# A transformer block on one core: fewer warming products, other ranks for an order written by hand, a table loaded first, and a last group in two banks

## The chip, the cores and the metric

The kernel runs on one core of one Trainium2 chip. The time is device microseconds (us) of one execution. Before the change the median of three runs is 572.95 us (572.05 to 573.83). A core has five engines with queues of their own: TensorE (PE), VectorE (DVE), ScalarE (ACT), GpSimd (POOL) and SyncE (SP), which here issues nearly all DMA transfers.

## The reference

The input `x` is 4 x 2048 x 256, float32. The block adds an attention-like part and then a feed-forward part (FFN), each on a normalized x:

```python
x = x + attn(layernorm(x))
x = x + ffn(layernorm(x))

# attn: u, v of 256 channels each
u, v = split(silu(xn @ uv_w))
a    = Toeplitz coefficients, 4096 lags x 256 channels, from a small network
y    = irfft(rfft(a) * rfft(v), n=4096)[:2048]
attn = (u * y) @ o_w

# the network: position -> 32 features
h = pos @ rpe_pos_w
for i in range(3):
    h = silu(ln(h)) @ rpe_fc_w[i]
a = silu(ln(h)) @ rpe_out_w          # times 0.99 ** |lag|

# ffn: 8 groups of 1024 tokens, each with its own weights, no function in between
h1 = x_g @ W1[g].T + b1[g]           # 256 -> 1024
h2 = h1 @ W2[g].T + b2[g]            # 1024 -> 256
```

As nothing stands between the two products of the FFN, the kernel multiplies W1 and W2 with each other first (`pw`, a 256 x 256 result per group, kept in `wt`) and then applies `wt` to the tokens (`pff`).

## The kernel before, in words

**An order written out by the kernel itself.** The stages don't call the engines. They call a `Recorder`, which notes every instruction as an `Operation` with a *rank*. `at(key, b)` sets the rank: `place(key, b)` looks the key up in the table `PLACE` (L156), which gives 20 x b plus the entry. For the first batch the key with " first" behind it goes ahead, for the last batch the key with " last". A key that is not there falls back to its parent: "w.3.l.1" to "w.3.l", that to "w.3", that to "w". When all is recorded, `issue_order` (L289) writes the order: it keeps a simple model of the time of each operation (`Operation.cost`), of the buffers of each pool, and again and again takes the operation that can start first by that model, of several the one of lowest rank. The result goes to the engines in that order, under `tc.manual_schedule()`. Each engine's queue then runs in order, and waits on semaphores where data or a buffer is missing. So a rank only moves instructions past each other within what the data and the buffers allow; and all recorded instructions have one line in the profile, L1166, and are told apart by their tiles.

**The stages**, for a batch b of 4, a quarter q of 4 (512 tokens each) and a half h of 2 (128 channels each):

- *Warming products*, keys "warm.i" (L1123): `zeros` (128 x 256) times itself, into the bank of `ps_w`; nothing reads the result. There are `WARM_UP` = 20 of them, and each has a rank of its own. A 128x256 float32 product is two instructions in the profile.
- `rpe_network` (keys "rpe...", L628): SP loads parameters, lags and the first two quarters of x that are used (q = 0 and 2); the two halves of quarter 0 go by ACT's queue. Then four layers, each in two halves k: the product `ph`, its square `sq` and copy `d` on ACT, the variances `pvar` (16 small products), three Newton steps for the inverse root on DVE (`nt`, `ny`), its spread `ne`, four transposes `pr`, a product with `d` on DVE, and Silu on ACT (`z`). Each step needs the one before it. Then `pz`, the last transposes.
- `stage_a` (keys "a.q..."): x is normalized (`xn_a`), transposed (`pt_a`, copied to `xnt` by ACT), multiplied (`pv`), Silu on ACT gives `v`, and POOL makes the sums and differences `c` of the convolution. For the first batch these fill PE while the network's steps wait on each other.
- `stage_w` (keys "w.g...", L854), for each of the 8 FFN groups: four pairs of loads `w1`, `w2` of 256 KB each ("w.g.l.i"), each in a ring of `WB` = 3 buffers; ACT adds a bias in place; then 8 instructions of `pw` for the pair ("w.g.m.i"). All 32 gather in one bank, as `ps_w` has a single one, and DVE takes it out to `wt` ("w.g.s"). A buffer comes free when `pw` has used it, and the next load then takes its place; the next group can start only when the bank is out.
- `rpe_transform` (keys "rpet..."): the network's result is transformed to the coefficients `am` that the convolution multiplies with: `hp`, then `pa`, row-tiled (products with 64 rows, at two `tile_position`s), 8 of them under each of the four keys "rpet.1.a" to "rpet.7.a".
- `prepare` ("p.h.n"): the butterflies of the convolution on DVE, ahead of `stage_b` ("f.h.r..." forward product `pf` and multiplication `y` with `am`; "b.h.r..." backward product `acc`; "e.h.n" the butterflies behind it, then the product with the gate on POOL). Its tables `mats` are loaded anew for each r, in rings of 3 buffers.
- `gate` ("g.h.q"): the product `pu` and its Silu.
- `stage_d` ("d.q...", L1068): `po` (the output projection), added to x, normalized, transposed (`pt_d`, copied to `xn` by ACT), the FFN's product `pff` in two groups j of 256 tokens, added to x by DVE, and stored. For the last batch the `pff` groups are in the two banks of `ps_i` (tag "acc"), and each group has a store of 256 KB of its own. Quarter 1 is the last to be done.

The eight PSUM banks are: `ps_f` 2, `ps_i` 2, `ps_w` 1, `ps_mm` 3. Silu and the simple functions of ACT (copy, square, identity) need a table, which the profile shows as ACT_TABLE_LOAD.

Of the kernel before, what the change touches and what calls it, by code (L numbers as in the profile page):

```python
# [31 lines left out]
F32 = mybir.dt.float32  # L32
I32 = mybir.dt.int32
AF = mybir.ActivationFunctionType
ALU = mybir.AluOpType
# [106 lines left out]
class Pool:  # L142
# [14 lines left out]
    "a.0": 1.74, "a.0.t": 0.0,  # L157
    "a.1": -2.67, "a.1.c": 26.0, "a.1.t": -5.0, "a.1.v": -1.3,
    "a.2": 2.51, "a.2.c": 101.0, "a.2.n": 6.0, "a.2.v": 3.0,
    "a.3": 5.3, "a.3.c": 31.0, "a.3.t": 4.46, "a.3.x": 1.0,  # L160
    "a.0.c first": -99.0, "a.0.n first": -160.0, "a.0.t first": -150.0, "a.0.v first": -122.0, "a.0.x first": -190.0, "a.0.w first": -142.0,
    "a.1 first": -98.0, "a.1.c first": -98.0, "a.1.t first": -112.0, "a.1.v first": -111.0,
    "a.2.c first": -124.0, "a.2.n first": -152.0, "a.2.t first": -120.0, "a.2.v first": -119.0,
    "a.2.x first": -140.0,
    "a.3 first": -96.0, "a.3.c first": -96.0, "a.3.t first": -104.0, "a.3.x first": -96.0,
    "b.0": 13.79, "b.0.0": 6.26, "b.0.0.p": 5.0, "b.0.1.m": 12.16, "b.0.1.p": 12.0, "b.0.1.y": 8.0, "b.0.2": 4.1,
    "b.0.2.y": 18.0, "b.0.3.m": 8.11, "b.0.3.p": 6.0, "b.0.3.y": 6.6, "b.0.4.m": 8.37, "b.0.4.p": 11.0,
    "b.0.4.y": 7.0, "b.0.6": 12.58, "b.0.6.p": 12.0, "b.0.7": 14.11, "b.0.7.y": 13.0,
    "b.1": 10.46, "b.1.0.p": 8.0, "b.1.1": 20.27, "b.1.1.y": 32.0, "b.1.2.m": 87.0, "b.1.2.p": 17.0,
    "b.1.2.y": 15.97, "b.1.3": 19.01, "b.1.3.p": 16.0, "b.1.4.m": 18.94, "b.1.4.p": 18.0, "b.1.4.y": 143.0,  # L170
    "b.1.5": 18.98, "b.1.5.y": 19.0, "b.1.6": 20.74, "b.1.6.p": 21.3, "b.1.7": 20.97, "b.1.7.p": 21.4,
    "b.0 last": 4.1, "b.0.0.p last": 2.0, "b.0.0.y last": 15.0, "b.0.1 last": 12.16, "b.0.1.p last": 7.3,
    "b.0.1.y last": 12.16, "b.0.2.y last": 4.1, "b.0.3.p last": 7.0, "b.0.3.y last": 6.0, "b.0.4.p last": 2.3,
    "b.0.4.y last": 2.0, "b.0.5.m last": 13.79, "b.0.5.p last": 7.1, "b.0.5.y last": 9.0, "b.0.6.p last": 12.58,
    "b.0.6.y last": 220.0, "b.0.7.y last": 20.0,
    "b.1 last": 27.0, "b.1.0.m last": 10.46, "b.1.0.p last": 7.0, "b.1.0.y last": 18.0, "b.1.1.m last": 77.0,
    "b.1.1.p last": 27.0, "b.1.1.y last": 120.0, "b.1.2 last": 15.97, "b.1.2.m last": 15.97, "b.1.2.p last": 15.97,
    "b.1.2.y last": 20.0, "b.1.3.p last": 20.7, "b.1.3.y last": 21.0, "b.1.4.p last": 20.0, "b.1.4.y last": 53.0,
    "b.1.5.y last": 27.0, "b.1.6.m last": 92.0, "b.1.6.p last": 32.7, "b.1.6.y last": 57.0, "b.1.7.p last": 47.0,
    "b.1.7.y last": 64.0,  # L180
    "d.w": -60.0,
    "d.0": 27.7, "d.0.n": 27.0, "d.0.o": 25.35, "d.0.x": 25.35,
    "d.1": 28.74, "d.1.n": 27.0, "d.1.o": 26.25, "d.1.x": 26.25,
    "d.2": 30.44, "d.2.f": 36.0, "d.2.s": 33.54, "d.2.t": 33.54,
    "d.3": 31.46, "d.3.n": 29.38, "d.3.o": 29.15, "d.3.x": 29.38,
    "d.0 last": 42.27, "d.0.f last": 111.0, "d.0.n last": 42.27, "d.0.o last": 97.0, "d.0.t last": 63.0,
    "d.0.x last": 42.27,
    "d.1 last": 140.66, "d.1.n last": 184.0, "d.1.o last": 145.0, "d.1.x last": 65.21,
    "d.2.f last": 59.0, "d.2.n last": 154.0, "d.2.o last": 100.0, "d.2.t last": 79.0, "d.2.x last": 46.22,
    "d.3.f last": 85.0, "d.3.n last": 178.0, "d.3.o last": 104.0, "d.3.t last": 100.0, "d.3.x last": 61.26,  # L190
    "e.0": 14.0, "e.0.0": 14.31, "e.0.1": 26.0, "e.0.3": 15.0, "e.0.4": 63.85, "e.0.5": 71.2, "e.0.6": 77.59,
    "e.0.7": 13.0, "e.0.10": 22.0,
    "e.1.0": 21.0, "e.1.1": 20.5, "e.1.2": 41.0, "e.1.3": 39.0, "e.1.4": 21.4, "e.1.5": 39.89, "e.1.6": 22.0,
    "e.1.7": 25.0, "e.1.8": 22.6, "e.1.9": 27.0, "e.1.10": 28.0,
    "e.0 last": 22.0, "e.0.1 last": 18.21, "e.0.2 last": 18.05, "e.0.3 last": 16.77, "e.0.7 last": 22.0,
    "e.0.9 last": 21.84, "e.0.10 last": 21.0,
    "e.1.0 last": 85.0, "e.1.1 last": 100.83, "e.1.2 last": 37.0, "e.1.3 last": 79.0, "e.1.4 last": 154.0,
    "e.1.5 last": 229.0, "e.1.6 last": 100.0, "e.1.7 last": 60.0, "e.1.8 last": 74.0, "e.1.9 last": 104.0,
    "e.1.10 last": 122.0,
    "f.0": 2.91, "f.0.0": 2.08, "f.0.0.p": 3.0, "f.0.2.m": 1.13, "f.0.2.p": -1.7, "f.0.2.y": 0.0, "f.0.3.m": 2.05,  # L200
    "f.0.3.p": -1.0, "f.0.3.y": 4.0, "f.0.4": 4.0, "f.0.4.p": 7.0, "f.0.5.m": 3.57, "f.0.5.p": 6.0, "f.0.5.y": 9.0,
    "f.0.6.m": 101.0, "f.0.6.p": 11.7, "f.0.6.y": 5.0, "f.0.7.m": 7.2, "f.0.7.p": 10.0, "f.0.7.y": 7.0,
    "f.1": 18.04, "f.1.0.m": 81.0, "f.1.0.p": 7.0, "f.1.0.y": 4.04, "f.1.1.m": 18.16, "f.1.1.p": 13.4,
    "f.1.1.y": 16.0, "f.1.2.m": 13.91, "f.1.2.p": 12.3, "f.1.2.y": 10.0, "f.1.3.m": 14.02, "f.1.3.p": 12.0,
    "f.1.3.y": 10.0, "f.1.4.m": 14.8, "f.1.4.p": 14.0, "f.1.4.y": 11.0, "f.1.5": 14.19, "f.1.5.y": 13.0,
    "f.1.6.m": 17.79, "f.1.6.p": 17.7, "f.1.6.y": 13.43,
    "f.0 last": 0.0, "f.0.0 last": 0.0, "f.0.0.m last": 2.08, "f.0.0.p last": 0.0, "f.0.1.m last": 2.91,
    "f.0.2 last": 1.13, "f.0.2.p last": 1.13, "f.0.2.y last": 4.0, "f.0.3 last": 2.05, "f.0.3.p last": 2.05,
    "f.0.3.y last": 2.05, "f.0.4.p last": 4.0, "f.0.4.y last": 3.0, "f.0.5.m last": 33.0, "f.0.5.p last": 7.0,
    "f.0.5.y last": 6.0, "f.0.6 last": 6.5, "f.0.6.m last": 6.5, "f.0.6.p last": 10.0, "f.0.6.y last": 6.5,  # L210
    "f.0.7.m last": 45.0, "f.0.7.p last": 9.4, "f.0.7.y last": 6.26,
    "f.1 last": 14.02, "f.1.0 last": 4.04, "f.1.0.m last": 4.04, "f.1.0.p last": 9.0, "f.1.1 last": 18.16,
    "f.1.1.p last": 20.3, "f.1.1.y last": 18.16, "f.1.2 last": 13.91, "f.1.2.p last": 12.0, "f.1.2.y last": 13.91,
    "f.1.3.p last": 14.02, "f.1.3.y last": 14.02, "f.1.4 last": 14.8, "f.1.4.p last": 14.8, "f.1.4.y last": 14.8,
    "f.1.5.y last": 16.0, "f.1.6.p last": 32.0, "f.1.6.y last": 24.0, "f.1.7.m last": 18.04, "f.1.7.p last": 52.0,
    "f.1.7.y last": 55.0,
    "g.0.0": 7.0, "g.0.1": 6.5, "g.0.2": 15.0, "g.0.3": 5.68,
    "g.1.0": 24.0, "g.1.1": 9.2, "g.1.2": 20.0, "g.1.3": 21.0,
    "g.0.0 first": -95.0, "g.0.1 first": 1.77, "g.0.2 first": -51.0, "g.0.3 first": -40.12,
    "g.1.0 first": -72.0, "g.1.1 first": -63.0, "g.1.2 first": -20.0, "g.1.3 first": -56.0,  # L220
    "p.0": 5.0, "p.0.0": 112.0, "p.0.1": 1.74, "p.0.2": 22.08, "p.0.3": 23.91, "p.0.4": 1.63, "p.0.5": 110.0,
    "p.0.6": 38.78, "p.0.8": 4.06, "p.0.9": 16.19, "p.0.11": 33.43, "p.0.12": 39.59, "p.0.13": 95.0, "p.0.14": 8.0,
    "p.0.15": 33.61,
    "p.1.0": 14.03, "p.1.1": 11.0, "p.1.2": 11.32, "p.1.3": 67.54, "p.1.4": 106.0, "p.1.5": 15.0, "p.1.6": 14.31,
    "p.1.7": 12.0, "p.1.8": 15.07, "p.1.9": 18.9, "p.1.10": 70.61, "p.1.11": 20.64, "p.1.12": 55.0, "p.1.13": 20.4,
    "p.1.14": 45.22, "p.1.15": 23.0,
    "p.0.0 first": 21.76, "p.0.1 first": -58.0, "p.0.2 first": -38.0, "p.0.3 first": -3.8, "p.0.4 first": -3.5,
    "p.0.5 first": -23.28, "p.0.6 first": -84.19, "p.0.7 first": -2.6, "p.0.8 first": -26.0, "p.0.9 first": -2.0,
    "p.0.10 first": -21.0, "p.0.11 first": -9.0, "p.0.12 first": -1.1, "p.0.13 first": -0.8, "p.0.14 first": -0.5,
    "p.0.15 first": -8.0,  # L230
    "p.1.1 first": 5.6, "p.1.4 first": 11.67, "p.1.5 first": 16.0, "p.1.7 first": 16.92, "p.1.8 first": 31.0,
    "p.1.10 first": 73.0, "p.1.12 first": 26.0, "p.1.15 first": 86.73,
    "rpe": -145.0,
    "rpe.0": -180.0,
    "rpe.1": -150.0,
    "rpe.2": -135.0,
    "rpe.3": -132.0,
    "rpe.d": -174.0,
    "rpe.s": -179.0,
    "rpe.v": -170.0,  # L240
    "rpe.z": -100.0,
    "rpet": -82.0,
    "rpet.0": -33.0, "rpet.0.m": -10.0,
    "rpet.1": -26.0, "rpet.1.a": -50.0, "rpet.1.m": -10.0,
    "rpet.2": -23.0, "rpet.2.m": -10.0,
    "rpet.3": -77.0, "rpet.3.a": -9.6, "rpet.3.m": -10.0,
    "rpet.4": -65.0, "rpet.4.m": -10.0,
# [1023 lines left out]
```

## Time and profile before

| | |
|---|---|
| median of 3 runs | 572.95 us (572.05, 572.95, 573.83) |
| the profiled execution | 572.52 us |
| its span, from the first instruction to the last | 570.6 us |
| granted TensorE clock over the span | 1.000 |
| first matmul starts | 1.19 us |
| last add on DVE starts | 567.02 us |
| DMA | 81.37 MB, mean 143 GB/s |
| `w` loads: 64 of 256 KB, median from issue to landing | 4.4 us |
| `mats` loads: 128 of 256 KB | 2.7 us |
| stores of 512 KB, 256 KB | 2.9 us, 2.0 us |

The busy time of the engines by stretches of the span, in us:

| stretch | what is in it | PE | DVE | ACT | POOL |
|---|---|---|---|---|---|
| 0 to 50 | the network, first stage a, groups 0 and 1 of w | 47.1 | 30.0 | 37.3 | 16.1 |
| 50 to 160 | the transform, gate, first convolution | 110.0 | 103.2 | 52.0 | 25.1 |
| 160 to 520 | the batches | 358.3 | 337.0 | 204.8 | 98.9 |
| 520 to 570.6 | last weights, last stage d | 45.1 | 35.1 | 17.7 | 9.8 |

How to read it: busy time of PE contains overlap of pipelined instructions, so a stretch with 110.0 of 110 us may still hold waits below a microsecond. A line of the timeline has the start, the duration from the first start to the last end of a row of like instructions, the engine, the line, the operation with its output and input tiles, how many, and in brackets the idle time ahead of it with what ended it.

### The profile page before, as it was taken

What the parts mean: (1) busy time and instruction counts of PE and PEld (TensorE: products, weight loads), DVE (VectorE), ACT (ScalarE), POOL (GpSimd) and SP (SyncE); (2) the same over time, 40 slices, a digit from 0 to 9 for tenths busy, and PEclk for the clock granted to TensorE, in tenths of its full rate; (3) what the DMA queues carried; (4) which work ended last, traced back from release to release, by engine and by line L of the source; (5) the groups of instructions that cost most, each with busy time, mean ns of one, the idle gap of its engine ahead of it and who ended that gap; (6) DMA issues with size and microseconds to landing.
All of it is one profiled execution on the core that took longest, in us unless ns stands there. A gap on an engine that the chain in (4) does not pass through costs nothing.

```text
span 570.6 us, 8345 instructions
## 1 busy us (share of the span) xinstructions
PE 560.5 (98%) x2676; PEld 459.8 (81%) x2676; DVE 505.3 (89%) x1122; ACT 311.7 (55%) x820; POOL 149.8 (26%) x184
## 2 busy tenths in 40 slices
PE   9999999999999999999999999999999999999997
PEld 6778667988887788888788788887887888878785
DVE  7646998999997999999968999999959999989963
ACT  3987772533333824868756618868568237112162
POOL 1245120020534320204473010316462021020410
PEclk9999999999999999999999999999999999999999
DMA  8832673544574326365251454545332553434212
GB/s 292 273 89 57 189 225 119 185 130 139 175 176 148 86 109 204 118 215 202 76 147 51 138 184 129 187 160 162 111 74 93 158 193 109 140 130 118 67 38 111
DMA packets 40483, 81.37 MB, mean 143 GB/s; under 512 B 5876, under 2 KB 7412, under 8 KB 40440
## 3 DMA queue, kind: packets, MB, share of 16 engines
q1 hardware_dynamic: 39960, 80.19, 45.4%
q10 hardware_dynamic: 480, 0.66, 0.3%
q8 instruction: 21, 0.34, 0.2%
q14 instruction: 22, 0.18, 0.1%
HBM read 72.44 MB, written 8.39 MB: 142 GB/s over the span
## 4 chain that ended last, share of the span: by engine, by line
PE 95%; DVE 2%; DMA 1%; ACT 1%; issue 0%; SPq 0%; ACTq 0%; DVEq 0%
PE acc L1166 18%; PE pf L1166 18%; PE pff L1166 10%; PE pu L1166 10%; PE po L1166 9%; PE pv L1166 9%; PE pw L1166 8%; PE pt_a L1166 2%; PE pt_d L1166 2%; PE warm L1166 2%; PE pa L1166 1%; DMA w<-in_L_ffn_W_dram 1%; PE hp L1166 1%; PE ph L1166 1%; PE pvar L1166 1%; PE pr L1166 1%
## 5 line engine op out<-in xcount | busy, mean ns | idle before, releaser
L1166 PE MATMUL acc<-mats,y 128*128 128x256 f32 (+1 forms) x512 | 114.5, 367 | 0.0
L1166 PEld LDWEIGHTS acc<-mats,y 128*128 128x128 f32 x512 | 91.8, 190 | 15.7 <-issue 3.9
L1166 POOL TENSOR_TENSOR gt<-gt,tk 128x512 f32<-128x512 f32 x32 | 44.9, 1416 | 114.9 <-DVE tk L1166 114.8
L1166 PE MATMUL pw<-w,w 128*128 128x256 f32 x256 | 62.5, 381 | 2.5 <-ACT w L1166 1.3
L1166 POOL TENSOR_TENSOR c<-v 128x256 f32<-128x256 f32 x64 | 51.3, 827 | 50.4 <-ACT v L1166 36.3
L1166 PE MATMUL pu<-xnt,uvw 128*128 128x512 f32 x128 | 61.0, 594 | 0.0
L1166 PE MATMUL pv<-uvw,xnt 128*128 128x256 f32 x256 | 61.0, 380 | 0.0
L1166 PE MATMUL po<-ow,gt 128*128 128x256 f32 x256 | 60.6, 380 | 0.3 <-DVE xd L1166 0.3
L1166 PE MATMUL pff<-wt,xn 128*128 128x256 f32 x256 | 59.5, 382 | 0.7 <-ACT xn L1166 0.7
L1166 PE MATMUL pf<-ra,mats 128*128 128x256 f32 x256 | 59.5, 379 | 0.0
L1166 PEld LDWEIGHTS pw<-w,w 128*128 128x128 f32 x256 | 46.7, 190 | 12.0 <-ACT w L1166 3.6
L1166 PEld LDWEIGHTS pff<-wt,xn 128*128 128x128 f32 x256 | 48.0, 190 | 8.4 <-ACT xn L1166 2.1
L1166 ACT ACTIVATE w<-w,dw 128x256 f32<-128x256 f32 x64 | 29.4, 501 | 46.1 <-DMA w<-in_L_ffn_W_dram 46.0
L1166 PEld LDWEIGHTS pv<-uvw,xnt 128*128 128x128 f32 x256 | 48.1, 190 | 7.8 <-issue 1.2
L1166 PEld LDWEIGHTS pf<-ra,mats 128*128 128x128 f32 x256 | 48.4, 190 | 7.1 <-PE po L1166 0.2
L1166 PEld LDWEIGHTS po<-ow,gt 128*128 128x128 f32 x256 | 47.5, 190 | 8.1 <-DVE xd L1166 1.2
L1166 DVE TENSOR_TENSOR y<-y,far 128x256 f32<-128x256 f32 x128 | 53.1, 453 | 0.1
L1166 POOL TENSOR_TENSOR rs_d<-ve_d,mhalf 128x4 f32<-128x4 f32 x16 | 19.0, 1188 | 113.0 <-ACT ve_d L1166 95.9
L1166 POOL TENSOR_TENSOR rs_a<-ve_a,mhalf 128x4 f32<-128x4 f32 x16 | 20.2, 1262 | 106.0 <-ACT ve_a L1166 92.2
L1166 ACT COPY e<-acc 128x512 f32<-128x512 f32 x24 | 14.0, 582 | 53.1 <-PE acc L1166 52.2
L1166 ACT ACTIVATE gt<-pu 128x512 f32<-128x512 f32 x32 | 19.0, 593 | 40.8 <-PE pu L1166 38.4
L1166 DVE TENSOR_TENSOR y<-pf,am 128x512 f32<-128x512 f32 x56 | 38.2, 682 | 3.5 <-PE pf L1166 3.4
(159 smaller groups left out, 1042.4 us busy)
## 6 DMA issues: line engine op xcount, KB each, us to landing
mats<-in_mats_dram SPq DMA_DIRECT2D x128, 256.0 KB, 2.7
w<-in_L_ffn_W_dram SPq DMA_DIRECT2D x64, 256.0 KB, 4.4
xa<-in_x_dram SPq DMA_DIRECT2D x16, 512.0 KB, 4.6
xd<-in_x_dram SPq DMA_DIRECT2D x14, 512.0 KB, 3.6
out_dram<-xd SPq DMA_DIRECT2D x12, 512.0 KB, 2.9
mats_rpe<-in_mats_dram SPq DMA_DIRECT2D x8, 256.0 KB, 4.5
row<-in_L_ffn_b_dram SPq DMA_DIRECT2D x8, 128.0 KB, 4.8
ph<-in_phases_dram SPq DMA_DIRECT2D x8, 128.0 KB, 5.1
```

Of the source, the lines that this page charges most:

```text
L1166: ops[k].call(*ops[k].args, **ops[k].kw)
```

## The change

There are four edits.

1. `WARM_UP` is 11 instead of 20: nine warming products fewer.
2. One ACTIVATE more, Silu of `eps` (128 x 1) into a tile that nothing reads. It has the rank of the first warming product, so it stands near the head of ACT's queue.
3. In `stage_d`, for the last batch, quarter 1, group j = 1: instead of one `pff` tile of two 256-column halves, one add and one store of 256 KB, there are two tiles (both of tag "acc"), each with its two products, its own add of 256 columns and its own store of 128 KB.
4. `PLACE` has 473 keys instead of 445: 177 keys have another value, 225 the same, 43 are gone and 71 are new.

```diff
-    "a.0.c first": -99.0, "a.0.n first": -160.0, "a.0.t first": -150.0, "a.0.v first": -122.0, "a.0.x first": -190.0, "a.0.w first": -142.0,
...
+    "a.0.c first": -99.0, "a.0.n first": -214.0, "a.0.t first": -158.0, "a.0.v first": -156.0, "a.0.w first": -142.0,
+    "a.0.x first": -190.0,
...
-    "rpe": -145.0,
+    "rpe": -152.0,
     "rpe.0": -180.0,
-    "rpe.1": -150.0,
-    "rpe.2": -135.0,
-    "rpe.3": -132.0,
+    "rpe.1": -175.0,
+    "rpe.2": -159.0,
+    "rpe.3": -150.0,
     "rpe.d": -174.0,
     "rpe.s": -179.0,
-    "rpe.v": -170.0,
+    "rpe.v": -240.0,
...
-    "rpet.1": -26.0, "rpet.1.a": -50.0, "rpet.1.m": -10.0,
...
-    "rpet.3": -77.0, "rpet.3.a": -9.6, "rpet.3.m": -10.0,
+    "rpet.1": -65.0, "rpet.1.a": -23.4, "rpet.1.m": -10.0,
...
+    "rpet.3": -59.0, "rpet.3.a": -22.0, "rpet.3.m": -10.0,
...
-    "w.3": 32.0, "w.3.l.0": -27.0, "w.3.l.1": 2.0, "w.3.l.2": 34.0, "w.3.l.3": 14.0, "w.3.m.1": 25.0, "w.3.m.2": 3.0,
-    "w.3.m.3": 21.0, "w.3.s": 36.0,
...
+    "w.3": 32.0, "w.3.l.0": 1.0, "w.3.l.1": 2.0, "w.3.l.2": 34.0, "w.3.l.3": 14.0, "w.3.m.1": -8.0, "w.3.m.2": 17.0,
+    "w.3.m.3": 21.0, "w.3.s": 3.0,
...
-COLD, IDLE, WARM_UP = 3500, 1800, 20
+COLD, IDLE, WARM_UP = 3500, 1800, 11
...
         for j in range(2):
+            if last and q == 1 and j == 1:
+
+                for i in range(2):
+                    t = 2 * j + i
+                    pf = ps_i.tile([P, D], F32, tag="acc", name=f"pff_{b}_{q}_{t}")
+                    for dt in range(2):
+                        T.matmul(pf, xn2[:, dt, t * P : (t + 1) * P], wt[:, dt, :], start=(dt == 0), stop=(dt == 1))
+                    V.tensor_tensor(xt[:, t, :], xt[:, t, :], pf, ALU.add)
+                    S.dma_start(out[b, q][:, t, :], xt[:, t, :])
+                continue
...
     V.memset(zeros, 0.0)
+
+    A.activation(const.tile([P, 1], F32, name="silu0"), eps, AF.Silu)
     warm = ps_w.tile([P, 2, D], F32, tag="w", name="warm")
```

The other ranks of `PLACE` that change belong to the same stages (a, b, d, e, f, g, p, rpe, rpet, w) and are not printed here. Since `issue_order` works on all operations at once, they move instructions throughout the program; the prediction names the places that matter to it, by the position of an instruction in its engine's order.

## The prediction

> **What bounds the kernel now.** I read the page first, then the chain of waits, then the timeline of each place where the chain leaves TensorE (PE), and last the order in which the changed program's instructions stand on each engine.
>
> ```profile
> span 570.6 us, 8345 instructions
> ...
> PE 560.5 (98%) x2676; PEld 459.8 (81%) x2676; DVE 505.3 (89%) x1122; ACT 311.7 (55%) x820; POOL 149.8 (26%) x184
> ...
> PE 95%; DVE 2%; DMA 1%; ACT 1%; issue 0%; SPq 0%; ACTq 0%; DVEq 0%
> ```
>
> The set-up is simple: 95% of the chain that ends last is PE. Time can only go away in two ways: fewer products, or fewer waits of PE. Busy PE is pipelined, so I count starts: in a stream, one 128x256 instruction starts every 0.216 us (16 of `pv` take 3.45 us in the chain of waits), a 128x512 one every 0.429, a 128x128 one every 0.109. By these prices all PE instructions of the old program make 549.6 us. From the first start (1.19) to the slot after the last (566.75) 565.6 us pass, so PE loses about 16 us; then 3.8 us of tail. Where the 16 are:
>
> ```profile
> 1.19 6.63 PE L1166 MATMUL warm<-zeros 128*128 128x256 f32 x20 [1.19 <-DVE zeros L1166]
> ...
> 14.48 1.28 ACT L1166 ACT_TABLE_LOAD   x1
> 15.77 1.52 ACT L1166 ACTIVATE z<-d,par 128x512 f32<-128x512 f32 x2
> ...
> 16.64 1.98 PE L1166 MATMUL ph<-z,bd 128*128 128x512 f32 x4 [1.07 <-ACT z L1166]
> ```
>
> The first 20 instructions of `warm` take 6.6 us instead of 4.3: the first ten run at half speed, the other ten at full speed. Then the network of four layers is a latency chain, and its second layer (`ph<-z,bd`) waits for Silu's table. The wait printed is 1.07; counted by starts it is 1.24, since the pipeline's end covers a part. At the third layer's `pr`, 0.29 and 0.65 us go the same way (starts at 38.3 and 39.5, behind DVE's `ne`).
>
> ```profile
> 173.52 7.56 SPq L1166 DMA_DIRECT2D w<-in_L_ffn_W_dram  x8
> ...
> 177.31 0.91 ACT L1166 ACTIVATE w<-w,dw 128x256 f32<-128x256 f32 x2 [7.62 <-DMA w<-in_L_ffn_W_dram]
> ...
> 178.25 1.97 PE L1166 MATMUL pw<-w,w 128*128 128x256 f32 x8 [1.34 <-ACT w L1166]
> ...
> 199.65 0.70 PE L1166 MATMUL pff<-wt,xn 128*128 128x256 f32 x2 [0.40 <-ACT xn L1166]
> ```
>
> A weight buffer's turn: PE lets it go at 173.3, SP issues the loads at 173.5, ACT adds the bias at 177.3, PE uses it at 178.25: 4.95 us. The order had put only 3.45 us of products in between (8 products, two instructions each), so PE waited 1.50. The `pff` at 199.65 had 0.44 us of products between its transposes and itself, and waited another 0.57.
>
> ```profile
> 526.43 5.95 PE L1166 MATMUL pw<-w,w 128*128 128x256 f32 x24 [0.43 <-issue]
> ...
> 533.10 1.97 PE L1166 MATMUL pw<-w,w 128*128 128x256 f32 x8 [0.71 <-DMA w<-in_L_ffn_W_dram]
> ```
>
> The last group of weights: 0.59 us until the single bank of `pw` is evacuated (two `po` products, 0.86 us, stood there as cover: the evacuation takes 1.45), then 0.19, 0.20 and 0.88 us for three buffers with 4.31, 4.31 and 3.45 us of products as cover. With the waits that fall into them, these turns took 4.7 to 5.3 us.
>
> **The change part by part.**
>
> *Nine products of zeros fewer.* 18 instructions at 0.216 = 3.88 us of PE work. In the new order ten products still stand ahead of `ph0` (so the warming up is as before) and one behind it; the nine that go stood between 9 and 27 us, where the chain of the network was waited for. They are worth 3.88 only if that chain gets shorter too.
>
> *The table, and the start's new order.* One load instead of two: 1.28 us less in ACT's queue right ahead of `z`. I followed the new order with the old rows' durations. Newton's steps for layer 0 are no longer mixed with three BN_STATS (0.42 each), so `ne` starts at 10.4 instead of 10.9; `pr` stands right behind the transposes, 11.3 instead of 12.6; two products with `d` (0.69) and `z` (0.81) follow, `z` at 12.8 instead of 15.8, `ph1` at 13.8, `pvar1` ends at 17.8 instead of 22.8. Layers 2 and 3 by the same rows (Newton 2.5, `ne` 0.68, `z` 0.81, two ACT copies and squares 0.5 each) bring `pz`, the network's end, to 48.5; it was at 54.7. Products ahead of `pz`: 42.5 us in the new order, 48.5 in the old. So PE loses 6.0 us up to there, before 6.2: the 1.24 of the table and that 0.94 at `pr` go, and new ones come where zeros had filled in: 0.5 ahead of the first transposes, 0.8 at `pv` of quarter 2 (0.44 of products as cover for a copy of 0.59 and two hops), 0.5 at `ph3`, and crumbs. One cost is new: Silu on `eps` and its table load now stand between the two loads of the first x on ACT's queue. Before, the second was issued at 1.19; now between 1.2 (if the queue runs past a table load) and 2.5. It landed 3.8 us after its issue, and DVE wants it at 5.66: 0 to 0.85 us late, and w0, `ph0` and the chain behind it with it. No row shows a DMA issue behind a table load; I take 0.4. Start: -0.2 + 0.4 = +0.2 (bounds -1.5 and +2).
>
> *Row-tiled products in fewer groups.*
>
> ```profile
> 74.56 0.59 PE L1166 MATMUL pw<-w,w 128*128 128x256 f32 x2
> 75.09 1.13 PE L1166 MATMUL pa<-wz,tr 64*128 64x256 f32 x8
> ```
>
> Going into `pa` and out again costs 0.39 us by starts (0.10 in, 0.20 inside, 0.10 behind). The old order does it five times, the new one three: -0.78.
>
> *Weight loads.* In the new order groups 3 and 2 are laid out otherwise: the covers in products are 5.60, 4.74, 9.48 and 4.74 us, and 1.29 for the evacuation. Against 4.95 and 1.45 these wait 0.2 three times: 0.6 instead of 1.50, -0.9. In the first 50 us one buffer has 5.16, enough if its turn is no longer than the 4.7 to 5.3 seen. At the end the evacuation has one product as cover, 0.43: it waits 1.02 instead of 0.59, and the buffers behind keep their waits, as their covers (3.88, 3.88, 3.45) and that wait together are the old ones: +0.43. The `pff` at 199.65 gets 1.30 us of cover: -0.57. The `mats` loads are covered by 3.9 us or more in both, but for one with 3.45 at 366; at 3.9 none waited: nothing taken.
>
> *The FFN's last group.*
>
> ```profile
> 565.30 0.69 DVE L1166 TENSOR_TENSOR xd<-xd,pff 128x512 f32<-128x512 f32 x1 [2.59 <-PE pff L1166]
> 567.02 0.69 DVE L1166 TENSOR_TENSOR xd<-xd,pff 128x512 f32<-128x512 f32 x1 [1.04 <-PE pff L1166]
> ```
>
> The last add works on 256 columns (0.41 for such an add out of PSUM at 200.46) instead of 512 (0.69): -0.28. The last store is 128 KB, issued as before from SP; 512 KB take 2.9 us, 256 KB 2.0, so 128 KB between 1.55 and 2.0, I take 1.85: -0.15. One more DMA (0.33 of SP) lies under the products. Against it: the third half-tile needs the bank that the add of 565.30 to 565.98 frees, and its slot was 565.89: +0.2. Sum -0.2 (bounds -0.6 and +0.1).
>
> *All other ranks* move equal work about. DVE is 95% busy from 60 to 160 us, so a stage there could turn DVE-bound; but its work begins with `pz`, 6 us earlier, and PE comes only 4 us earlier. A new wait can cost 0 to 3 us in all; taken 0.5.
>
> Sum: -3.88 + 0.2 - 0.78 - 0.9 - 0.57 + 0.43 - 0.2 + 0.5 = -5.2. The profiled execution took 572.52 (its span and 1.9 around it) and becomes 567.3; the median of the runs is 572.95, 0.43 more: 567.7.
>
> **The Trainium skill.** "ScalarE: Activation LUTs", section "What ACT_TABLE_LOAD costs", gives about 1283 ns for the load and some 1380 ns of drain, an estimate of 2.66 us per switch; here the load is 1.283, but `z` starts 0.01 us behind it, so by the page the sum would be 1.4 us lower, and the trace speaks against it. "TensorE: Matmul & The Clock Gate", section "Why this matters for your kernels", warns of gaps over about 3 us, which bring the half clock back; that speaks against taking zeros out, though no gap in this trace is longer than 1.5 us.
>
> **The rivals.**
> 1. *The zeros only filled waits.* If the network's chain holds `pz` at 52.4 or later, the 3.88 is not gained: 567.7 + 3.9 = 571.6. For it: the zeros stood just where PE had nothing. Against: the chain loses the table, three BN_STATS and the zeros themselves from ahead of `pr` and `pvar`.
> 2. *Slower: weight buffers come late.* The new order uses four buffers with covers of 4.7 to 5.6 us where the old had 11 or more, and PE and ACT stand behind each in order. While the load queue is deep, the first weights took 6.6 to 7.5 us to land (issued 5.42, landed 12.78). With a turn of 7 us instead of 4.95 the four wait 1.8 + 1.4 + 2.3 + 2.3 = 7.8 instead of 0.6: 567.7 + 7.2 = 574.9. It decides from a turn of 6.3 on. Against: by 50 us the old queue had run empty, and turns at 173 and 520 took 4.7 to 5.3.
> 3. *Half clock again at the start.* With gaps between 9.6 and 13 us the clock might fall; instructions then start every 0.427 instead of 0.216 as at 1.19 to 5.3, where it cost 2.1 us: 569.8. Against: the gaps are 0.5 us each.
> 4. *Better:* the new waits of the start and of the rest do not come (-0.2 - 0.4 - 0.5 - 0.6 more): about 565.5.
>
> **How the numbers follow.** Forecast (566 to 569.5) 0.55; better 0.17; half clock, or the late second half of x in full (569.5 to 571.2) 0.11; zeros gain nothing 0.09; slower 0.08. A measurement of this kernel tells about 0.3% (1.7 us) from no change: faster 0.83, same 0.10, slower 0.07. The range reaches from the better case, with the start's lower bound, 564.3, to rival 1, 571.6; it leaves out the slower case.
>
> **What would show it.** `pz` near 48.5 and one table load; `ph1` waiting for z by less than 0.3; three groups of `pa`; waits under 0.5 at the `pw` of groups 2 and 3 near 165; 1.0 us ahead of `pw` near 520; the last store near 1.85 us. `pz` after 52, or a wait over 1.5 at a `pw`, would show it wrong.

## The result, and the profile after

| | before | after |
|---|---|---|
| median | 573.0 us (572.05 to 573.83, 6 runs) | 569.6 us (568.75 to 570.41, 6 runs) |
| ratio of the medians, 95% interval | | 0.9932 [0.9919, 0.9945] |
| the profiled execution, its span | 572.52, 570.6 us | 568.75, 567.0 us |

The change makes the kernel 3.4 us faster. I had predicted 567.7, that is 5.2 less than before.

First the page of the changed kernel: the span, the busy time of the engines and the chain that ended last.

```profile
span 567.0 us, 8316 instructions
...
PE 557.0 (98%) x2658; PEld 455.7 (80%) x2658; DVE 504.5 (89%) x1123; ACT 309.5 (55%) x820; POOL 153.5 (27%) x184
...
PE 77%; DVE 11%; DMA 6%; ACT 3%; issue 1%; SPq 1%; ACTq 0%; DVEq 0%
```

PE has 18 instructions fewer, but the chain that ends last is only 77% PE now, where it was 95%. The chain follows a wait back through the load or the DVE work that ended it, so this share says where the chain passes and not how long PE waited: PE is busy for 98% of the span in both. How long PE waited is counted by starts below.

The timeline of ACT and of PE at the start, in the changed kernel:

```profile
1.19 1.28 ACT L1183 ACT_TABLE_LOAD   x1 [1.19 <-PEq L1272]
1.26 0.38 ACTq L1183 DMA_DIRECT2D xa<-in_x_dram  x1
2.48 0.20 ACT L1183 ACTIVATE silu<-eps 128x1 f32<-128x1 f32 x1
```

```profile
13.60 1.88 PE L1183 MATMUL ph<-z,bd 128*128 128x512 f32 x4
...
48.24 1.04 PE L1183 MATMUL pz<-ident,z 128*128 128x128 f32 x8
```

The last two lines are of PE. The row of `pz` in the kernel before:

```profile
54.70 1.04 PE L1166 MATMUL pz<-ident,z 128*128 128x128 f32 x8
```

There is one table load, and `ph` of the second layer has no wait in brackets any more. `pz`, the end of the network, starts at 48.24 (predicted 48.5, before 54.70). The second load of x stands behind the Silu in ACT's order, but it is issued at 1.26, while the table is still loading (1.19 to 2.47).

To see where the rest went I count what PE has lost at a place: the start of an instruction, less the work that stands ahead of it in PE's order at the prices of the prediction. The column "difference" is what the stretch adds to the loss after, less what it adds before. A place is good to about 0.1 us, since it depends on the prices.

| stretch | loss before, at its ends | loss after, at its ends | difference | predicted |
|---|---|---|---|---|
| products of zeros (work, not loss) | | | -3.88 | -3.88 |
| start to `pz` | 0 to 6.19 | 0 to 5.75 | -0.44 | +0.2 |
| to behind the last group of `pa` | 6.19 to 8.62 | 5.75 to 8.00 | -0.18 | -0.78 |
| to the end of the first batch's `acc` | 8.62 to 9.12 | 8.00 to 9.32 | +0.82 | rest, +0.5 |
| to the first `acc` of batch 1, h = 1 (groups 2 and 3, the `pff` at 199) | 9.12 to 11.63 | 9.32 to 10.51 | -1.32 | -1.47 |
| to `acc` r = 5 of the last convolution | 11.63 to 13.32 | 10.51 to 12.28 | +0.08 | rest |
| to behind the start of the last `acc` | 13.32 to 13.37 | 12.28 to 13.48 | +1.15 | rest |
| `pw` of group 7 | 13.37 to 15.45 | 13.48 to 16.03 | +0.47 | +0.43 |
| to the last quarter's `pff` | 15.45 to 17.06 | 16.03 to 17.38 | -0.26 | rest |
| from there to the end of the span | 7.38 us | 7.33 us | -0.05 | -0.2 |
| around the span | 1.95 us | 1.79 us | -0.16 | 0 |
| sum | | | -3.77 | -5.2 |

Of the -0.44 at the start, 0.27 is the start of `ph` of layer 0 alone (7.48 for 7.75), which depends on when the half rate at the start ends; from there to `pz` the loss fell by 0.17. The wait for a weight buffer near 166 and the wait for the evacuated bank near 523 stand in PE's timeline after:

```profile
166.07 1.97 PE L1183 MATMUL pw<-w,w 128*128 128x256 f32 x8 [0.68 <-DMA w<-in_L_ffn_W_dram]
...
523.12 3.77 PE L1183 MATMUL pw<-w,w 128*128 128x256 f32 x16 [0.88 <-issue]
```

The largest line that I had not foreseen is the last `acc`. The timeline of ACT and of PE there, after:

```profile
515.80 0.91 ACT L1183 ACTIVATE w<-w,dw 128x256 f32<-128x256 f32 x2 [14.78 <-DMA w<-in_L_ffn_W_dram]
516.62 0.56 ACT L1183 COPY e<-acc 128x512 f32<-128x512 f32 x1
```

```profile
515.29 1.03 PE L1183 MATMUL pw<-w,w 128*128 128x256 f32 x4
517.23 1.99 PE L1183 MATMUL acc<-mats,y 128*128 128x256 f32 x8 [0.92 <-ACT e L1183]
```

and the timeline of ACT in the kernel before:

```profile
518.32 0.58 ACT L1166 COPY e<-acc 128x512 f32<-128x512 f32 x1 [8.08 <-PE acc L1166]
520.25 0.91 ACT L1166 ACTIVATE w<-w,dw 128x256 f32<-128x256 f32 x2 [1.35 <-DMA w<-in_L_ffn_W_dram]
```

ACT took these instructions in the order in which they stand. Before, the copy `e` out of the bank of `acc` stood ahead of the bias addition; in the new order it stands behind it. The bias waits for its load until 515.8, while the `acc` that `e` copies had its last product started at 515.1. The next `acc` waits for `e`. By starts this costs 1.08 and another 0.11 for the pipeline to fill.

### The profile page after: what moved, and what is told of

It is laid out like the page before. It is cut to its first block, busy times and chain, and to the rows that moved or that the text cites. A ratio compares the mean times of both kernels' runs of the same rounds, so it can differ in the third digit from the quotient of the medians.

```text
span 567.0 us, 8316 instructions
## 1 busy us (share of the span) xinstructions
PE 557.0 (98%) x2658; PEld 455.7 (80%) x2658; DVE 504.5 (89%) x1123; ACT 309.5 (55%) x820; POOL 153.5 (27%) x184
## 4 chain that ended last, share of the span: by engine, by line
PE 77%; DVE 11%; DMA 6%; ACT 3%; issue 1%; SPq 1%; ACTq 0%; DVEq 0%
PE acc L1183 15%; PE pf L1183 15%; PE pff L1183 10%; PE po L1183 10%; PE pu L1183 7%; PE pv L1183 7%; PE pw L1183 6%; DMA w<-in_L_ffn_W_dram 4%; DVE y L1183 3%; DMA xa<-in_x_dram 2%; PE pt_d L1183 2%; PE pt_a L1183 2%; DVE far L1183 1%; ACT w L1183 1%; SPq L1183 1%
## 5 line engine op out<-in xcount | busy, mean ns | idle before, releaser
L1183 POOL TENSOR_TENSOR c<-v 128x256 f32<-128x256 f32 x64 | 53.1, 858 | 39.7 <-ACT v L1183 33.4
L1183 PE MATMUL pf<-ra,mats 128*128 128x256 f32 x256 | 61.3, 379 | 0.0
L1183 DVE TENSOR_TENSOR far<-pf,am 128x512 f32<-128x512 f32 x56 | 38.1, 681 | 0.0
L1183 ACT ACTIVATE xn_d<-xd,nb_d,rs_d 128x256 f32<-128x256 f32 x56 | 29.5, 590 | 14.6 <-DVE nb_d L1183 12.2
```

The costliest lines, as they stand in the source:

```text
L1183: ops[k].call(*ops[k].args, **ops[k].kw)
```

## The experiments

For most of these kernels the order is computed as in the kernel named and then frozen: single instructions are left out, added or moved, and all other instructions of all engines keep their places. Where the source itself is changed instead (the early Silu put in or left out, the one bank), the order is computed anew, and again all other instructions keep their places:

```diff
+    order = issue_order(ops, tags)
+    def find(engine, name): ...        # in order, by the name of the tile written
+    def move(ks, anchor, behind=False): ...
     with tc.manual_schedule():
-        for k in issue_order(ops, tags):
+        for k in order:
```

Each ratio is to the kernel before, run beside it on the same chip; the medians of before were 573.2 (first group), 574.62 (second), 572.8 (third) and 574.48 (last).

| kernel | median, runs | ratio to before, 95% interval | span of its profile |
|---|---|---|---|
| old order, nine zeros left out | 574.8 (12) | 1.0017 [1.0002, 1.0032] | 571.3 |
| old order, early Silu | 572.03 (11) | 0.9975 [0.9965, 0.9986] | 571.2 |
| old order, both | 572.09 (11) | 0.9981 [0.9971, 0.9991] | 570.2 |
| changed, without the early Silu | 570.66 (7) | 0.9957 [0.9942, 0.9973] | 567.9 |
| changed, copy `e` first | 568.31 (5) | 0.9896 [0.9873, 0.9920] | 567.4 |
| changed, nine zeros back | 572.43 (12) | 0.9965 [0.9951, 0.9979] | 571.7 |
| changed, one bank | 569.86 (6) | 0.9919 [0.9896, 0.9942] | 569.4 |
| changed, six moves | 565.63 (4) | 0.9852 [0.9827, 0.9878] | 563.9 |
| changed, once more | 569.58 (5) | 0.9944 [0.9931, 0.9958] | 568.1 |
| six moves, once more | 566.86 (5) | 0.9895 [0.9878, 0.9912] | 564.5 |
| old order, nine zeros left out, second profile | 571.26 (1) | | 569.4 |
| six moves, eight warming products | 566.08 (4) | 0.9854 [0.9828, 0.9879] | 564.5 |

### What the zeros were worth in the old order

```diff
+    for k in find("PE", "warm")[11:]:
+        order.remove(k)
```

> The old order as it is, with only the nine products of zeros left out that stand behind the first network layer. My theory (the network's chain holds, zeros are worth only what of them stands in its path): `pr` of layer 0 starts when `ne` is there, about 11.6 instead of 12.6 us, `pvar` of layer 1 gains one zero more, `pr` of layer 1 waits for `ne` again; `pz` moves from 54.7 to about 53.0 and the time falls by 1.4 to 1.9 us. Rival A (every product of zeros counts): 3.9 us less, `pz` at 50.8. Rival B (they only filled waits): 0 to 0.4 us less, `pz` where it was.

Measured: not faster at all, but slower by 0.17%. Two lines of PE's timeline of this kernel, and one stretch of its table by windows (the last columns: granted clock, share and rate of DMA):

```profile
10.77 0.93 PE L1183 MATMUL pt_a<-ident,xn_a 128*128 128x128 f32 x4 [0.44 <-ACT xn_a L1183]
11.54 1.75 PE L1183 MATMUL pr<-ident,ne 128*128 128x128 f32 x8
```

```profile
12.00:14.00 2.00, 2.00 (x11) 1.91 (x10) 1.87 (x6) 0.42 (x2) 0.00 (x0) 0.50 1.03 381
```

`pr` takes 1.75 for eight where it took 1.04 before. The granted clock is 0.50 from 12 to 14, and by their starts products run at half rate from about 11.7 to 15.1. So this was the rival "half clock again", in a kernel where I had not expected it: a gap of 0.44 us, where zeros had stood, came ahead of it. A second profile of the same kernel:

> The old order without the nine zeros, one more look, for the clock alone. Its first profile had a gap of PE of 0.44 us at 10.3 and then 4 us at half the clock (11.3 to 15.2), which the same order with the early table load did not have after the same gap. If the gap brings the half clock down for sure, it is there again; if it depends on where the gap falls, it may be missing, and `ph` of layer 1 is then 0.9 to 1.2 us earlier than 9.0 us behind `ph` of layer 0.

```profile
11.75 1.05 PE L1183 MATMUL pr<-ident,ne 128*128 128x128 f32 x8
```

The same gap of 0.44 is there (ahead of 10.99), and the half clock is not. `ph` of layer 1 then starts 8.10 behind `ph` of layer 0 instead of 9.00, and `pz` is at 53.65: 1.05 earlier than before, for 3.88 us of work less. The other 2.8 are waits where the zeros stood. That is the theory's kind, and less than its size (1.7).

The mean granted clocks of all executions show how often the half clock came. A stretch of 3.4 us at half the clock takes 0.003 off the mean of such an execution. Eleven of the twelve executions behind the median lie at 0.993 to 0.997, five of them at 0.994 or less, which is about two such stretches. The twelfth has 1.000 and is the fastest, 571.88; the second profile (0.999) ran in 571.26. The two at the full clock are 1.3 and 1.5 us below the medians of the kernel before beside them, 573.2 and 572.8; the eleven have a median of 574.81, 1.6 above. So the nine zeros had two uses in the old order: they filled waits, and with them the clock stayed up (0.999 or more in all thirty executions of the kernel before beside it). Two executions at the full clock are few, and the start alone moves an execution by a microsecond, so the 1.3 and 1.5 are rough. Not all of the slowness is explained: among executions with 0.997 the times go from 573.20 to 575.17, and in the first profile a wait of 1.2 at `pt_a` near 293, which the second does not have, makes a part.

### The table, and both

```diff
+    A.activation(const.tile([P, 1], F32, name="silu0"), eps, AF.Silu)
```

> The old order as it is, with only the early Silu added: one table load near 1.2 us instead of one there and one ahead of `z`. My theory: `z` starts 1.28 earlier, the wait of `ph` at 16.64 (1.24 by starts) goes, nothing behind it fills the gap again: 1.2 us less. The second half of x is issued at 1.3, past the table load, as in the changed kernel (I had counted 0.4 us of delay). Rival (the wait is taken over by the next late thing, the copy of the transposes or the squares): under 0.5 us less.

> Both edits of the start on the old order. If the two are independent, the sum of the two runs above (2.6 to 3.1 by my theory). If they help each other, since each shortens a chain that the other one leaves as the bound: up to 3.9. What is left between this kernel and the changed one is then the ranks and the last group: by these numbers about 0.7 us, of which the tail alone makes 0.3.

The table alone brings 0.25% [0.14, 0.35], about 1.4 us, as expected; `pz` moves from 54.70 to 53.73 although `ph` of layer 0 starts 0.37 later, so the chain behind it is 1.34 shorter. Both together bring no more than the table alone. In the profile `pz` is another 0.99 earlier (52.74) and the span 1.0 shorter; the medians show nothing of it. But nine of these eleven executions have a mean clock of 0.996 or 0.997 again (median 572.43); the two at the full clock, the profiled one among them, took 572.09 and 571.14. So the test of the two together is mixed up with the half clock. On the old order leaving out the nine zeros is worth about 1 us of the chain where the clock stays up, and nothing or less where it falls.

> The changed kernel without the early Silu, all engines' orders otherwise the same: the table load stands ahead of the first `z` again. My theory: the new start has no slack at `ph` of layer 1, so 1.0 to 1.3 us more, `pz` at 49.3 to 49.5 instead of 48.2. Rival (the new order gave `z` room): under 0.4 more.

Measured 570.66 (ratio 0.9957, the changed kernel 0.9932 and 0.9944). `ph` of layer 1 waits 1.21 as in the old kernel, and `pz` is 42.00 behind `ph` of layer 0 instead of 40.76. The new start has no slack there: the table is worth 1.2 to 1.3 us of the chain on both orders. Two of these seven executions, with 0.996 and 0.997, show the half clock too.

### The zeros in the new order

```diff
+    # nine more products of zeros, ahead of pt_a (3), pr of layer 0, pvar of layer 1, pv of quarter 2 (2), pr of layer 1 (2)
+    order[i:i] = extra[:n]
```

> The changed kernel with nine products of zeros put back on PE, ahead of the same transposes and products as in the old order; all other engines' orders are the changed kernel's. On the old order the nine were worth only about 1.0 us of the start (3.88 of work less, 2.9 of waits more). Theory: in the new order the chain is shorter, and they would be paid nearly in full: 2.4 to 3.2 us more. Rival (the new order still has room where the zeros stood): under 1.2 more.

Measured 572.43, beside 569.86 for the changed kernel with one bank on the same chip: 2.6 more. The changed kernel itself was not run beside it; by its own two ratios (0.9932 and 0.9944 against 0.9965) it is 1.2 to 1.9. In the profile `pz` comes 43.35 behind `ph` of layer 0 instead of 40.76: 2.59 later. So in the new order the nine zeros cost 2.6 of their 3.88 on the chain, in the old one at most 1.0. The gain is neither the zeros' nor the ranks' alone: the ranks shorten the chain, and only then are the zeros in its way. Nor does the new order need them for the clock: it is 0.999 or more in all eleven executions of the changed kernel. With the nine zeros back the new ranks, the table and the last group together (0.9965) take little more off than the table alone on the old order (0.9975); a kernel with the new ranks alone was not run.

### The copy behind the bias

```diff
+    move(find("ACT", "e6_3_1_"), find("ACT", "w1_6_6_")[0])
```

> The changed kernel with one instruction moved: on ACT's queue the copy `e` out of the bank of `acc` (r = 6 of the last convolution) stands ahead of the two bias additions of the last weight pair of group 6, where it stood behind them. Theory: the 1.19 us that the last `acc` loses near 517 come from that place in ACT's queue, since the bias waits for a load (it had been the only thing ACT had to do) and the copy behind it: the wait falls under 0.15 us, and the time by 0.9 to 1.2. Rival (the bank or the table of `acc` is late for another reason, DVE's reads or the `mats` load): the wait stays over 0.8 us.

ACT's and PE's timelines of this kernel:

```profile
516.90 0.59 ACT L1199 COPY e<-acc 128x512 f32<-128x512 f32 x1 [14.51 <-PE acc L1199]
517.38 0.91 ACT L1199 ACTIVATE w<-w,dw 128x256 f32<-128x256 f32 x2
```

```profile
517.54 1.99 PE L1199 MATMUL acc<-mats,y 128*128 128x256 f32 x8
```

The copy runs when its `acc` is done, and the last `acc` starts without a wait in brackets; one moved instruction takes 0.0023 off the ratio against the kernel with one bank beside it (568.31 against 569.86, though the intervals overlap). The place in the queue is the cause, and not the bank or a table. It is shown by the line, and the time alone would not show it: in five profiles of the new order with the copy behind the bias this `acc` waited 1.0 to 1.9 us, and here it does not wait.

### The last group

```diff
-            if last and q == 1 and j == 1:
-                ... two tiles, two adds, two stores
-                continue
```

> The changed kernel with the old last group: one bank, one add of 512 columns, one store of 256 KB. By the two traces the stretch from the last add to the end of the span is 3.28 us with the new group and 3.58 with the old one, and the new one's second tile waits 0.15 us for a bank. So 0.2 to 0.4 us more by the profile's tail; less than the times can tell surely.

The last add of the changed kernel and of this one, in DVE's timeline:

```profile
563.72 0.42 DVE L1183 TENSOR_TENSOR xd<-xd,pff 128x256 f32<-128x256 f32 x1 [0.70 <-PE pff L1183]
```

```profile
565.88 0.69 DVE L1173 TENSOR_TENSOR xd<-xd,pff 128x512 f32<-128x512 f32 x1 [1.04 <-PE pff L1173]
```

From the add's start to the end of the span 3.24 us pass after the change and 3.55 here. But from the first product of the last quarter's `pff` to the end of the span it is 7.33 with the two banks and 7.38 with one: the last add comes 0.25 later behind that first product (4.08 for 3.83), since the second tile waits for the bank that an add still holds, and this takes nearly all of the gain back. The span's other 2.4 us come from elsewhere: 0.93 from the start and 1.2 from `pa` and `hp` near 77 and 82, which waited that long in no other profile of this order.

### Six moves, and eight warming products

```diff
+    move(find("ACT", "e6_3_1_"), find("ACT", "w1_6_6_")[0])
+    move(find("PE", "po_3_0_0_")[:1], find("PE", "po_3_0_1_")[0])
+    move(find("PE", "pv_1_3_1_"), find("PE", "pw_2_")[4])
+    move(find("PE", "pv_0_3_1_")[3:], find("PE", "pr3_1_")[0])
+    move(find("ACT", "w1_1_2_")[:1], find("ACT", "xnt_0_2_")[1], True)
+    move(find("ACT", "w1_0_2_")[1:], find("ACT", "w1_0_2_")[0], True)
```

> The changed kernel with six moves in the frozen order, each at a wait of its trace: the copy `e` as in the first kernel of this group (1.1 us expected); a product of `po` put next to the other as cover for the evacuation of `pw` at 522 (0.43, perhaps less as the gate's product on POOL is due just behind); four `pv` ahead of the `pw` that waits for its load at 166 (0.8); a `pv` ahead of the `pr` at 46.0 (0.4); a bias addition behind the two copies `xnt` at 19.3 (0.25); a bias addition ahead of the gate's Silu at 53.8 (0.37). Sum 3.3; expected 2.0 to 3.3 less than the changed kernel, which would be about 567 us. Rival (each wait moves to the next late thing): under 1.2.

> The changed kernel once more, on one chip with the next run, so that the two can be compared. From eleven profiles the half-clock stretch at the start ends between 4.6 and 7.2 us and `ph` of layer 0 starts between 7.3 and 8.6 us whatever the kernel; so I expect its `ph` in that band, `pz` 40.8 us behind `ph` (as in its first profile), and the wait of the last `acc` near 517 at 1.0 to 1.2 us again.

> The kernel with six moves once more, beside the changed kernel on the same chip: 2.5 to 3.5 us less than it (from 7.32 us behind the first of the last quarter's `pff` to the end, as before; the wait of the last `acc` under 0.15; the `pw` near 166 under 0.2).

On one chip the changed kernel took 569.58 and this one 566.86: 2.7 us less, inside the expected 2.5 to 3.5. By starts, the wait of the last `acc` went (1.2), that of `pw` at 166 too (0.85), that of the evacuation fell from 1.04 to 0.61, of `pr` at 46 from 0.66 to 0.23, of `pv` at 20.8 from 0.65 to 0.45. One move did nothing: `pw` at 55 still waits 0.40. Its other load, `w2`, landed only at 54.33, so the place of the bias had not been the last thing. The kernel with six moves is faster than both kernels of this case.

> The kernel with six moves, with two of the ten warming products ahead of `ph` of layer 0 left out as well. In the profiles so far ten of them end when the half rate of the start lets them: `ph` starts between 7.28 and 8.63 us, while its weights `w0` are ready at 6.9. With eight, `ph` starts at 7.0 to 7.05 where the rate rises early and at 7.9 at the latest: 0.3 to 0.9 us less than the kernel with six moves, and less spread between executions. Rival (the rate rises later or falls back in the gap ahead of `ph`): `ph` itself or the products behind it run at half rate, 1 us more or worse.

```profile
7.43 1.98 PE L1206 MATMUL ph<-lag_t,w 4*128 4x512 f32 x4
```

In this execution the half rate lasted to 6.5, nearly as long as in the late ones (6.7 to 6.8). `ph` started at 7.43, where ten warming products had put it at 8.41 to 8.46 in three of those late executions. The time, 566.08, lies between the two medians with ten, on another chip: whether the whole kernel gains is not shown.

## Why the prediction was right, and where it was short

- *Direction and range* were right: 569.6 lies in 564.3 to 571.6. It is just above the band of the forecast (566 to 569.5) and in the one that I had given to the half clock or a late second half of x, and neither of them happened. The forecast itself was 1.9 us too low. Of that 1.43 are steps of the sum, and 0.42 is the way from the profiled execution to the median, which I had taken as 0.43 as before and which was 0.85: the profiled execution was the fastest of its six.
- *"They are worth 3.88 only if that chain gets shorter too"* held, and the runs show it from both sides: at most 1.0 of the chain on the old order, 2.6 on the new one. What I had not seen is that the zeros also held the clock up in the old order.
- *The start* (+0.2) was better, -0.44. The step that was mis-sized is the late second half of x: I had taken 0.4 between 0 and 0.85, and it was 0, as the queue issues the load during the table's. The other term, -0.2, was right for the chain itself: -0.17 from `ph` of layer 0 to `pz`. The remaining -0.27, and with it `pz` at 48.24 instead of 48.5, is luck: the half rate ended earlier in this execution. In the second profile of the changed kernel `ph` starts at 8.45 and `pz` at 49.20, and the start costs 0.5 more than before.
- *Row-tiled products* (-0.78): the stretch gave -0.18, but not for want of this gain. By starts, with 0.108 us for one of these products, a row of 8 or of 16 costs 0.40 above its work, the rows of 18 and 14 in the old order 0.61 each, and the row of 32 in the new one 0.65. In all 2.41 became 1.45, -0.96, so I had priced the term too low, as I had put every row at 0.39. (In the kernel before, the sixteen at 94.34 take 1.93 up to the next start, the eight at 75.09 take 1.06: both are 0.20 above their work, and the ends cost the other 0.20.) Two new waits took the gain back. The weight buffer at 55 with 5.16 us of cover, which I had called enough, waited 0.44 with the pipeline's filling; its second load took 4.8 us to land. And `hp` near 80 waited 0.34 for DVE.
- *Weights and evacuation* held: -1.32 for -1.47 near 170 and 200, +0.47 for +0.43 at group 7. The sum is right in part by luck: of the three small waits expected (0.6 in all) only one came, but it was 0.85 instead of 0.2, with a turn of 5.6 us.
- *The last group* (-0.2): -0.05. The add and the store were as priced (0.42 and 1.86 us); the wait for the bank was 0.25 instead of 0.2 and the gain behind it 0.31 instead of 0.43.
- *"All other ranks"* (+0.5) is the term that was furthest off: it was +1.79, the four rows "rest" of the table together. I had bounded it by 0 to 3 and taken 0.5 without going through the order on ACT, though that order was known. I had followed PE's covers for every weight buffer, and not what stands *behind* a bias that waits for its load: 1.15 at the last `acc`. 0.8 more came at `acc` near 133 and 155; the row at 155 names DVE for its wait.
- *The rivals.* The zeros did not only fill waits, in this order; in the old one they nearly did. In the first profile no weight buffer that PE waited for had a turn beyond 5.6 us (the wait at the evacuation aside), where the slower case decides from 6.3. The half clock did not come back in any of the eleven executions of the changed kernel, but did in eleven of thirteen of the old order without the zeros.

## What to carry to other kernels

Filler work on the busiest engine costs only as far as it delays the chain behind it: take it away together with what shortens the chain, and measure the two both singly and together. Read the granted clock of every execution when you take filler away, not of the profiled one alone: the filler may be what keeps the clock up. When an order changes, go through the queues of *every* in-order engine for instructions that wait on a load, and read what stands behind each; a copy that frees a bank must not stand there. A profile's own time can lie off the median by a term of the start alone, so compare two profiles from a common event behind the warming up.

## What the runs showed of the hardware

The half rate at the start ends at its own time, not after a number of products. PE's first rows of the changed kernel in its two profiles, the first execution:

```profile
1.19 6.36 PE L1183 MATMUL warm<-zeros 128*128 128x256 f32 x20 [1.19 <-DVE zeros L1183]
7.48 1.98 PE L1183 MATMUL ph<-lag_t,w 4*128 4x512 f32 x4
```

and the second:

```profile
1.18 7.33 PE L1183 MATMUL warm<-zeros 128*128 128x256 f32 x20 [1.18 <-DVE zeros L1183]
8.45 1.98 PE L1183 MATMUL ph<-lag_t,w 4*128 4x512 f32 x4
```

The same 20 instructions take 6.36 or 7.33 us, and `ph` and all that follows starts 0.97 later; the two spans differ by 1.1. Over thirteen profiles with ten warming products ahead, `ph` started between 7.28 and 8.63. The profile's granted clock reads 1.00 in this stretch, although products start every 0.425 us instead of 0.216, as the traces hold no record of the clock before its first rise; in the later stretch of the kernel without zeros it read 0.50. In these records the first rise comes between 4.4 and 7.2 us. In the first profile of the kernel without zeros the clock is full from 4.88, half from 11.71 and full again from 15.12 us: it changed at multiples of 3.41 us from the first rise.

The Trainium skill, "TensorE: Matmul & The Clock Gate", section "Part 1: The HAM clock gate (the "warmup" mystery)", says that the clock follows a free-running window of activity and that the moment of the change therefore varies by 500 ns to either side; here it varied by 2.7 us in all, and the start of `ph` by 1.35. Its section "Why this matters for your kernels", which I had set against the change, has the half rate return after idle gaps of more than about 3 us. Here it returned behind a gap of 0.44 us in the one profile that shows it, and the mean clocks show a half clock, though not its place, in most executions of the old order without the nine zeros; the measurement decides, and gaps far below 3 us were not safe there. The same page, section "Part 4: PE-mode transpose", adds that transposes don't count as busy in the same way; the gap here did lie among transposes (`pt_a`, `pr`), where zeros had stood between them, but no run tells whether that was the reason.
